# A first batch in halves for sixteen steps only, with the seven-product down projection for all batches

## The chip, the cores and the metric

The kernel runs on one core of a Trainium2 chip. The core has a matrix engine (TensorE, in the profile PE, with its weight loads as PEld), a vector engine (VectorE, DVE), a scalar engine (ScalarE, ACT), a general engine (GpSimd, POOL) and a queue that issues most of the DMA transfers (SyncE, SP). Each engine works through its own instructions in the order in which the program issues them, and waits where an operand isn't there yet. The metric is the device time of one execution in microseconds (us); lower is better. All data are 32-bit floats.

## The reference

There are 8 batches of 512 tokens with 128 channels. Each goes through a linear attention with four heads, and then through eight dense experts that all see every token:

```python
x = x + layernorm(attention(layernorm(x)))      # attention adds its own input, and w_out, b_out
x = x + layernorm(experts(layernorm(x)))

# attention(x): xn = layernorm(x) * gamma + beta; q, k, v = split(xn @ w_qkv)
#   k = softmax(k, axis=tokens); context = k^T v per head; out = (q * 32**-0.5) context
#   return out @ w_out + b_out + x
# experts(x): for wg, wu, wd in the 8 experts:
#   acc += (silu(x @ wg) * (x @ wu)) @ wd       # 128 -> 512 -> 128 channels
```

An expert has 512 hidden channels, so that the eight together make 32 slices of 128. A "step" of the kernel is one such slice for one batch.

## The kernel before

**Steps.** The main loop (lines 962 to 1019) runs over units. A unit is a batch, or half of one, and a range of steps. In a step PE makes `g` (line 976) and `u` (line 978) from the batch's transposed input `zT`, ACT makes `sg`, the Silu of `g` (line 980), and DVE makes `h = sg * u` (line 994, in the last units line 988). `g` and `u` have two PSUM banks each (`ps_gu`), so PE can run ahead of DVE by two steps and no more.

**Down projection.** In units that hold a whole batch, two steps make a pair, and the pair's 2x2 block product is done with seven products in place of eight. POOL makes the needed differences of `h` in the tile `t2` (lines 1014 to 1016, three instructions for a pair), and the sums of the weights were made once into `ws` (`weight_sums`, POOL, line 801). Eight pairs form a group; its products (`down_pairs`, line 863) are issued two steps after the group's last step, on two halves of PE's columns at once, into the banks accA and accB. When a batch's last group is done, `Last` adds the pieces up, in the next batch's steps.

**First batch.** It runs as two units of 256 tokens, each through all 32 steps: 64 half-steps. Its down projection is the plain one (`down`, line 811): one product for each half-step into one bank. At the end of a unit `fT` is copied (line 817) and `finish` (lines 703 to 715) transposes it on PE (line 259), normalises and stores.

**Opening.** Before the loop, `opening` (lines 304 to 428) computes the first batch's attention with all engines, in halves. It runs `after_wa` (lines 660 to 701) as two generators, `first` and `second`: y in PSUM, its statistics (`norm_stats`), `yn`, the residual `x2`, statistics of `x2`, `z`, the transposes and `zT`. `first` is run to its end, since the loop's first g needs its half of zT. `second` is carried on in the loop's first steps. Products called `unread` (`keep_warm`, line 165) fill PE meanwhile.

**Other batches' attention.** For batches from the third on it goes in stages, methods of the class `Attention` (lines 510 to 597), which `plan` (lines 873 to 935) places at numbered steps: for example `keys` at step 1, `context` at 4 to 7, `norm4` and `turn4` at 17. It transposes in 32x32 blocks on DVE and carries the blocks to their places through DRAM, with SP issuing one store and four loads each time (`carry`). The second batch is different: the generator `attention` (lines 430 to 475) gives it one piece at each step of the first batch's second unit, with transposes on PE. `prepare` (lines 143 to 159) and `weight_sums` run in the same way in the first unit.

**Order.** The order of instructions on each engine is the order of the program text, since the schedule is manual. In a step it is: `g`, `u`, Silu, `h`, the calls that `between` (lines 937 to 957) has for this step, the down products that are due, the differences `t2`.

**End.** The last batch runs 24 steps as a whole and the other 8 steps in halves. `End` (lines 717 to 777) adds a half's products token-wise into one PSUM bank. Both tiles of the last half are normalised together in `finish` (lines 753 to 777).

Of the kernel before, what the change touches and what calls it, by code (L numbers as in the profile page):

```python
# [16 lines left out]
def kernel(  # L17
# [40 lines left out]


# [28 lines left out]

    WHOLE, HALVES = [(0, NJ)], [(0, NJ // 2), (NJ // 2, NJ)]
# [21 lines left out]

    wg_sb, wu_sb, wd_sb = [], [], []
    for e in range(E):
        g = const.tile([P, F], F32, name=f"wg_{e}")
        nc.sync.dma_start(g, wg[e])
        u = const.tile([P, F], F32, name=f"wu_{e}")
        nc.sync.dma_start(u, wu[e])
        d = const.tile([P, NF, C], F32, name=f"wd_{e}")
        nc.sync.dma_start(d, wd[e].rearrange("(f p) c -> p f c", p=P))
        wg_sb.append(g)  # L120
        wu_sb.append(u)
        wd_sb.append(d)
        if e == 0 and B > 1:
            xs[1] = load_x(1)

    warm = const.tile([P, N // 2], F32, name="warm")
    nc.vector.memset(warm, 1.0)
# [15 lines left out]
    def prepare():  # L143


        wq_ps = ps.tile([P, N], F32, tag="ps", name="wq_ps")
        nc.tensor.transpose(wq_ps[:, :C], w_qkv_sb[:, 0:C], ident)
        nc.scalar.mul(wqT, wq_ps[:, :C], QSCALE)
        nc.scalar.mul(gwv, w_qkv_sb[:, 2 * C : 3 * C], gamma_sb)
        bv_ps = ps.tile([P, N], F32, tag="ps", name="bv_ps")  # L150
        nc.tensor.matmul(bv_ps[:, :1], w_qkv_sb[:, 2 * C : 3 * C], beta_sb, start=True, stop=True)
        bv = const.tile([P, 1], F32, name="bv")
        nc.scalar.copy(bv, bv_ps[:, :1])
        bvw = const.tile([P, C], F32, name="bvw")
        nc.scalar.mul(bvw, w_out_sb, bv)
        yield
        mb_ps = ps.tile([P, N], F32, tag="ps", name="mb_ps")
        nc.tensor.matmul(mb_ps[:, :C], heads, bvw, start=True, stop=True)
        nc.scalar.copy(mb, mb_ps[:, :C])
# [14 lines left out]
    def norm_stats(src, name):  # L174
# [13 lines left out]
        return mv, rstd  # L188

    def pair_stats(src, name):  # L190
# [15 lines left out]
        if n < NJ:  # L206
            nc.gpsimd.tensor_tensor(rstd[:, n:], ve[:, n:], mhalf[:, :n], ALU.pow)
            return mv, rstd[:, :n], rstd[:, n:], ve
        nc.gpsimd.tensor_tensor(rstd, ve, mhalf, ALU.pow)  # L209
        return mv, rstd[:, :n], rstd[:, n:]  # L210

    def bn(src, name):
        stats = small.tile([P, NJ, 6], F32, tag=f"stats{NJ}", name=f"stats_{name}")
        for j, t in enumerate(pieces(src)):
            nc.vector.bn_stats(stats[:, j, :], t)
        return stats

    def scales(stats, name, pair=False):


# [11 lines left out]
        for i in range(0, n, NJ):  # L232
            nc.vector.tensor_scalar(nm[:, i : i + NJ], mv[:, :, 0], -1.0, None, ALU.mult)  # L233
        rstd = small.tile([P, n], F32, tag=f"srstd{n}", name=f"rstd_{name}")
# [12 lines left out]
    def norm_apply(dst, src, mv_rstd):  # L247
        mv, rstd = mv_rstd
        for j in range(src.shape[1]):
            nc.vector.tensor_scalar(  # L250
                dst[:, j], src[:, j], mv[:, j, 0:1], rstd[:, j : j + 1],
# [47 lines left out]
    def parts(b):  # L299
        return HALVES if b == 0 else WHOLE  # L300

    x2s, zTs, rest = {}, {}, []

    def opening():
# [4 lines left out]
        def bank(name, tag):  # L309
# [13 lines left out]
        y = {}  # L323
# [6 lines left out]
        m = work.tile([P, C], F32, tag="m", name="m_0")  # L330
        first, second = [
            after_wa(b, lo, hi, xt, qT, m, x1b, x2, y, yn, z, zT) for lo, hi in HALVES
# [6 lines left out]
        keep_warm(warm, 4)  # L339
        keep_warm(w_qkv_sb[:, : N // 2])  # L340
        nc.scalar.copy(junk, warm[:, :1])
        s1 = [pair_stats(xt[:, J[h]], f"1_0_{h}") for h in H]
# [60 lines left out]
        nc.scalar.mul(qT[:, COL[0]], q_ps[0][:, :W], QSCALE)  # L403
        ctxT = work.tile([P, C], F32, tag="ctxT", name="ctxT_0")
# [8 lines left out]
        nc.vector.reciprocal(rsum, ksum[:, 2:3])  # L413
        nc.vector.tensor_scalar(m, m_ps[:, :C], rsum, None, ALU.mult)
# [3 lines left out]
        keep_warm(flat(xt[:, J[0]]), 2)  # L418
        next(first)
        next(first)  # L420
        keep_warm(flat(yn[:, J[0]]), 2)
        next(first)
        keep_warm(flat(x2[:, J[0]]), 2)
        next(first)
        next(second)
# [3 lines left out]

    def attention(b):  # L430

        xt = xs[b]
        mv, r1, r2 = pair_stats(xt, f"1_{b}")
        yield
        xh = work.tile([P, NJ, C], F32, tag="xh", name=f"xh_{b}")
        norm_apply(xh, xt, (mv, r2))
        yield
        yield
        xnT = work.tile([P, N], F32, tag="xnT", name=f"xnT_{b}")
        xh_ps = transpose4(flat(xh), f"xh_ps_{b}")  # L440
        nc.scalar.activation(xnT, xh_ps, AF.Identity, bias=beta_sb, scale=gamma_sb)
        yield
        k_ps = ps.tile([P, N], F32, tag="ps", name=f"k_ps_{b}")
        nc.tensor.matmul(k_ps, w_qkv_sb[:, C : 2 * C], xnT, start=True, stop=True)
        kmax = small.tile([P, 1], F32, tag="kmax", name=f"kmax_{b}")
        nc.vector.tensor_reduce(kmax, k_ps, AX.X, ALU.max, negate=True)
        ekT = work.tile([P, N], F32, tag="ekT", name=f"ekT_{b}")
        ksum = small.tile([P, 1], F32, tag="ksum", name=f"ksum_{b}")
        nc.scalar.activation(ekT, k_ps, AF.Exp, bias=kmax, accum_out=ksum)
        yield  # L450
        x1 = work.tile([P, NJ, C], F32, tag="x1", name=f"x1_{b}")
        norm_apply(x1, xt, (mv, r1))
        rsum = small.tile([P, 1], F32, tag="rsum", name=f"rsum_{b}")
        nc.vector.reciprocal(rsum, ksum)
        x1b = x1
        for j in range(NJ):
            nc.gpsimd.tensor_tensor(x1b[:, j, :], x1[:, j, :], bias_sb, ALU.add)  # L457
        yield
        ek = work.tile([P, NQ, P], F32, tag="ek", name=f"ek_{b}")
        ek_ps = transpose4(ekT, f"ek_ps_{b}")  # L460
        nc.vector.tensor_copy(
            ek.rearrange("p b (j k) -> p j b k", j=NJ),
            ek_ps.rearrange("p (j b k) -> p j b k", j=NJ, b=NQ),
        )
        yield
        yield
        yield from to_wa(b, xh, ek, rsum)
        wa = was[b]
        x2 = xp.tile([P, NJ, C], F32, tag="x2", name=f"x2_{b}")
        x2s[b] = x2  # L470
        y = work.tile([P, NJ, C], F32, tag="y", name=f"y_{b}")
        yn = y
        z = work.tile([P, NJ, C], F32, tag="z", name=f"z_{b}")
        zT = zp.tile([P, NQ, NJ, Q], F32, tag="zT", name=f"zT_{b}")
        yield from after_wa(b, 0, NJ, xt, xnT, wa, x1b, x2, y, yn, z, zT)

    was = {}
# [32 lines left out]
    class Attention:  # L510
# [27 lines left out]
        def keys(self):  # L538
# [12 lines left out]
            self.x1 = work.tile([P, NJ, C], F32, tag="x1", name=f"x1_{b}")  # L551
# [40 lines left out]
        def turn4(self):  # L592
# [3 lines left out]
            for lo, hi in parts(b):  # L596
                zTs[b, lo] = zT[:, :, lo:hi]
# [62 lines left out]
    def after_wa(b, lo, hi, xt, xnT, wa, x1b, x2, y, yn, z, zT):  # L660
        r = slice(lo, hi)
        pool, tag = (ps_gu, "u") if b == 0 and lo else (ps, "ps")
        y_ps = pool.tile([P, N], F32, tag=tag, name=f"y_ps_{b}_{lo}")
        if b == 0:
            for j in range(lo, hi):
                cols = slice((j - lo) * C, (j - lo + 1) * C)
                nc.tensor.matmul(y_ps[:, cols], ident, x1b[:, j, :], start=(j == lo), stop=False)
            yield
        for j in range(lo, hi):
            nc.tensor.matmul(  # L670
                y_ps[:, (j - lo) * C : (j - lo + 1) * C], xnT[:, j * P : (j + 1) * P], wa,
                start=(b > 0), stop=(b > 0 or j == hi - 1),
            )
        if b == 0:
            y[lo] = y_ps[:, : (hi - lo) * C].rearrange("p (j c) -> p j c", c=C)
            yb = y[lo]
        else:
            yb = y[:, r]
            nc.vector.tensor_tensor(flat(yb), y_ps[:, : (hi - lo) * C], flat(x1b[:, r]), ALU.add)
        yield  # L680
        s3 = norm_stats(yb, f"3_{b}_{lo}")
        yield
        norm_apply(yn[:, r], yb, s3)
        (nc.gpsimd if b or lo else nc.vector).tensor_tensor(
            flat(x2[:, r]), flat(yn[:, r]), flat(xt[:, r]), ALU.add
        )
        yield
        yield
        s4 = norm_stats(x2[:, r], f"4_{b}_{lo}")
        yield  # L690
        norm_apply(z[:, r], x2[:, r], s4)
        yield
        yield
        z_ps = transpose4(flat(z[:, r]), f"z_ps_{b}_{lo}")
        for j in range(hi - lo if b == 0 and lo == 0 else 1):
            cp = nc.vector.tensor_copy if j else nc.scalar.copy
            if b or lo:
                cp(zT[:, :, r], by_block(z_ps[:, : (hi - lo) * P], hi - lo))
            else:
                cp(zT[:, :, j], z_ps[:, j * P : (j + 1) * P].rearrange("c (a i) -> c a i", a=NQ))  # L700
        zTs[b, lo] = zT[:, :, r]

    def finish(b, lo, hi, fT):

        r = slice(lo, hi)
        n = hi - lo
        f_ps = transpose4(fT, f"f_ps_{b}_{lo}")
        f3 = f_ps.rearrange("p (j b k) -> p j b k", j=NJ, b=NQ)[:, :n]
# [253 lines left out]
    for n, (b, lo, hi, begin, end) in enumerate(units):  # L962
# [55 lines left out]
        for _ in others:  # L1018
            pass
# [36 lines left out]
```

## Time and profile before

Three runs took 704.2, 704.26 and 705.94 us, with a median of 704.26.

| what | value |
|---|---|
| the profiled execution | 705.33 us |
| its span, first to last instruction | 703.5 us |
| around the span | 1.8 us |
| mean granted clock of PE | 0.997 |
| first `g` of the loop starts | 20.34 us |
| first `g` of the second batch | 114.75 us |
| PE's last twelve product instructions start | 696.30 us |
| DVE `h` over 512 tokens, mean of one | 0.688 us |
| DVE `h` over 256 tokens, mean of one | 0.419 us |
| ACT Silu over 512 and 256 tokens, mean of one | 0.598 and 0.383 us |
| POOL power of 2, 4 and 8 columns, mean of one | 0.70, 1.02 and 1.64 us |
| POOL weight sum, 128x128, mean of one | 0.458 us |

A line of the profile's groups has the source line, the engine, the operation, output and inputs by the program's names, shapes and the count; then the busy time in us and the mean of one in ns; then the engine's idle time before it and what ended that. A line of the timeline has the start and the duration in us, the instruction, the count of merged ones, and in brackets the engine's idle time before it with what ended it. A line of the waits has who waited, for whom, the us in total, how often, and the longest. A matmul on 32-bit floats appears as two instructions, so x2 is one product. Durations of matmuls overlap, as they are pipelined; the distance between starts is what one costs in a full stream.

### The profile page before, as it was taken

Reading aid. Unit: us, or ns where it says so; the run is one execution under the profiler, and the core shown is the slowest. Engines: PE = TensorE matmul, PEld = TensorE weight load, DVE = VectorE, ACT = ScalarE, POOL = GpSimd, SP = SyncE. Lnnn points to the kernel's source line nnn. Section 1 sums busy time; section 2 is a strip of 40 time slices with the busy share of each in tenths; the row PEclk is TensorE's granted clock in tenths of the full one; section 3 lists DMA queues with packets and bytes.
Section 4 is the critical chain, followed back from the end, with each engine's and each line's share of the span. In section 5 each row is a group of like instructions: output and inputs, shape, how many; then the busy total and the mean of one; then the engine's idle time right before and its main releaser. Section 6 shows DMA issues by size and latency. Waiting matters only on the chain.

```text
span 703.5 us, 9130 instructions
## 1 busy us (share of the span) xinstructions
PE 690.5 (98%) x3161; PEld 397.5 (56%) x3161; DVE 297.5 (42%) x815; ACT 243.8 (35%) x472; POOL 386.1 (55%) x481
## 2 busy tenths in 40 slices
PE   8998999999999999999999999999999999999996
PEld 6787886455464545545455454555445454544576
DVE  5534463553424633364324634256242543235134
ACT  3332435324423434143342433324342323122221
POOL 3711120875737767385754857367663766546521
PEclk9999999999999999999999999999999999999999
DMA  8400001102011110202001020111101010020010
GB/s 266 157 1 0 8 0 51 32 1 75 0 48 43 54 39 20 63 8 89 1 31 60 2 91 0 31 60 32 46 0 65 26 47 1 0 61 1 15 56 20
DMA packets 33214, 28.19 MB, mean 40 GB/s; under 512 B 3600, under 2 KB 25360, under 8 KB 33168
## 3 DMA queue, kind: packets, MB, share of 16 engines
q1 hardware_dynamic: 32880, 27.41, 12.2%
q8 instruction: 25, 0.41, 0.3%
q10 hardware_dynamic: 288, 0.20, 0.1%
q14 instruction: 21, 0.17, 0.1%
HBM read 17.11 MB, written 10.49 MB: 39 GB/s over the span
## 4 chain that ended last, share of the span: by engine, by line
PE 94%; issue 2%; DVE 2%; POOL 1%; ACT 1%; DVEq 0%; POOLq 0%
PE g L976 31%; PE u L978 30%; PE accA L863 13%; PE accB L863 10%; PE acc L811 3%; PE acc L733 1%; PE y_ps L566 1%; PE g_ps L483 1%; PE k_ps L541 1%; PE unread L165 1%; POOL rstd L187 0%; DVE stats L181 0%; PE z_ps L259 0%; POOL x L457 0%; POOL rstd L209 0%
## 5 line engine op out<-in xcount | busy, mean ns | idle before, releaser
L994 DVE TENSOR_TENSOR h<-sg,u 128x512 f32<-128x512 f32 (+1 forms) x280 | 175.1, 626 | 356.2 <-PE u L978 340.9
L980 ACT ACTIVATE sg<-g 128x512 f32<-128x512 f32 (+1 forms) x296 | 159.5, 540 | 393.1 <-PE g L976 371.3
L976 PE MATMUL g<-zT,wg 128*128 128x512 f32 (+1 forms) x592 | 270.6, 539 | 0.9 <-DVE zT L700 0.7
L978 PE MATMUL u<-zT,wu 128*128 128x512 f32 (+1 forms) x592 | 268.9, 536 | 0.2 <-DVE h L994 0.2
L1014 POOL TENSOR_TENSOR t<-h 128x512 f32<-128x512 f32 x108 | 137.4, 1272 | 140.6 <-DVE h L994 140.6
L978 PEld LDWEIGHTS u<-zT,wu 128*128 128x128 f32 x592 | 112.4, 190 | 108.7 <-issue 100.9
L976 PEld LDWEIGHTS g<-zT,wg 128*128 128x128 f32 x592 | 107.9, 191 | 91.7 <-issue 86.2
L863 PE MATMUL accB<-t,ws 128*64 128x256 f32 x432 | 120.4, 381 | 0.0
L863 PE MATMUL accA<-h,wd 128*64 128x256 f32 x432 | 111.6, 381 | 0.0
L1016 POOL TENSOR_TENSOR t<-h,t 128x256 f32<-128x256 f32 x108 | 78.6, 727 | 8.5
L1015 POOL TENSOR_TENSOR t<-h,t 128x256 f32<-128x256 f32 x108 | 78.5, 727 | 8.5
L863 PEld LDWEIGHTS accA<-h,wd 128*64 128x64 f32 x432 | 58.0, 137 | 39.3 <-issue 5.6
L863 PE MATMUL accA<-t,ws 128*64 128x256 f32 x216 | 64.2, 379 | 0.0
L863 PE MATMUL accB<-h,ws 128*64 128x256 f32 x216 | 64.2, 379 | 0.0
L863 PEld LDWEIGHTS accB<-t,ws 128*64 128x64 f32 x432 | 58.0, 137 | 0.0
L235 POOL TENSOR_TENSOR rstd<-ve,mhalf 128x4 f32<-128x4 f32 (+1 forms) x24 | 28.1, 1171 | 23.0 <-DVE nm L233 15.6
L811 PE MATMUL acc<-h,wd 128*128 128x256 f32 x128 | 38.6, 383 | 0.0
L863 PEld LDWEIGHTS accB<-h,ws 128*64 128x64 f32 x216 | 29.6, 137 | 15.6
L863 PE MATMUL accB<-t,wd 128*64 128x256 f32 x108 | 32.1, 379 | 0.0
L863 PE MATMUL accA<-t,wd 128*64 128x256 f32 x108 | 32.1, 379 | 0.0
L187 POOL TENSOR_TENSOR rstd<-ve,mhalf 128x2 f32<-128x2 f32 (+1 forms) x9 | 7.0, 773 | 41.9 <-DVE ve L185 41.7
L863 PEld LDWEIGHTS accA<-t,ws 128*64 128x64 f32 x216 | 29.6, 137 | 0.0
(189 smaller groups left out, 455.9 us busy)
## 6 DMA issues: line engine op xcount, KB each, us to landing
wg<-in_L_ffn_Wg_dram SPq DMA_DIRECT2D x8, 256.0 KB, 6.0
wu<-in_L_ffn_Wu_dram SPq DMA_DIRECT2D x8, 256.0 KB, 5.9
wd<-in_L_ffn_Wd_dram SPq DMA_DIRECT2D x8, 256.0 KB, 6.1
x<-in_L_attn_x_dram SPq DMA_DIRECT2D x7, 256.0 KB, 3.1
bounce<-f_blkA SPq DMA_DIRECT2D x7, 256.0 KB, 2.0
fA<-bounce SPq DMA_DIRECT2D x28, 64.0 KB, 2.0
bounce<-f_blkB SPq DMA_DIRECT2D x7, 256.0 KB, 2.1
fB<-bounce SPq DMA_DIRECT2D x28, 64.0 KB, 2.0
```

What stands on the lines that cost most here:

```text
L165: nc.tensor.matmul(t[:, : moving.shape[1]], moving[:, :P], moving, start=(i == 0), stop=(i == count - 1),)
L235: nc.gpsimd.tensor_tensor(rstd, ve, mhalf[:, :n], ALU.pow)
L483: nc.tensor.matmul(g_ps[:, :C], xh[:, j, :], ek[:, :, j * Q : (j + 1) * Q], start=(j == 0), stop=(j == NJ - 1),)
L811: nc.tensor.matmul(accs[n][:, :cols], wd_sb[e][:, f, :], h, start=(i == 0), stop=(i == NSTEP - 1))
L863: nc.tensor.matmul(o, w, r, start=start, stop=stop)
L976: nc.tensor.matmul(g_ps[:, :cols], wg_sb[e][:, w], zT, start=True, stop=True)
L978: nc.tensor.matmul(u_ps[:, :cols], wu_sb[e][:, w], zT, start=True, stop=True)
L980: nc.scalar.activation(sg[:, :cols], g_ps[:, :cols], AF.Silu)
L994: nc.vector.tensor_tensor(h, sg[:, :cols], u_ps[:, :cols], ALU.mult)
L1014: nc.gpsimd.tensor_tensor(t2[:, 0:2], h2[:, 1::2], h2[:, 0:2], ALU.subtract)
L1015: nc.gpsimd.tensor_tensor(t2[:, 2], h2[:, 3], t2[:, 0], ALU.subtract)
L1016: nc.gpsimd.tensor_tensor(t2[:, 3], h2[:, 2], t2[:, 2], ALU.subtract)
```

## The change

1. The units of the first batch become: each half through steps 0 to 15, then the whole batch through steps 16 to 31.
2. Its down projection is by pairs with seven products. The first group's pairs are filled by both halves (`h2s`), the differences are made when the second half's step is there, and the group's products come after step 17. `down`, `finish` and `by_block` copies of `fT` are gone; `Last` finishes the batch in the second batch's steps.
3. In the half-steps, which have no down product, every third step takes accA and accB for `g` and `u`.
4. The second batch's attention is an `Attention` as well. Its statistics are made in `opening`; the stages are placed in the first batch's steps. x of the second batch is loaded ahead of the experts' weights. `bias` is split off from `keys`.
5. `prepare` runs in `opening`, in one bank. Weight sums of experts 0 to 4 are on POOL at steps 2, 4, 6, 8, 10; those of 5 to 7 on DVE at step 17.
6. `after_m` takes the variance of `x2` from the variances of its two parts and their covariance, instead of a second pass of statistics over `x2`.
7. The last half's two tiles have a bank each (accA, accB), and their normalisation goes tile by tile.
8. The constant 1.0 takes the place of the tile `warm`, and the first `keep_warm` makes five products.

```diff
+    xs[1] = load_x(1)
     for e in range(E):
...
-        if e == 0 and B > 1:
-            xs[1] = load_x(1)
-    warm = const.tile([P, N // 2], F32, name="warm")
-    nc.vector.memset(warm, 1.0)
+    warm = nc.const_aps.tensor(1.0, (P, N // 2), F32)
...
+        after = attentions[1] = Attention(1)            # in opening, after qT of half 0
+        after.s = bn(after.x[:, :3], "1_1")
...
+        bn(after.x[:, 3:], "1_1", after.s, 3)           # ahead of m
...
-        keep_warm(flat(xt[:, J[0]]), 2)
+        moment = moments(after.s, "1_1", pair=True)
+        weights = prepare()
+        next(weights)
+        keep_warm(flat(xt[:, J[0]]))
         next(first)
+        next(weights)
+        keep_warm(flat(xt[:, J[0]]))
         next(first)
-        keep_warm(flat(yn[:, J[0]]), 2)
+        next(weights)
         next(first)
-        keep_warm(flat(x2[:, J[0]]), 2)
-        next(first)
-        next(second)
+        after.sc = powers(*moment, "1_1")
+        keep_warm(flat(yn[:, J[0]]), 2)
+        next(first)
         for _ in first:
             pass
         rest.append(second)
...
+        mvx, vex = s1[h][0], s1[h][3]                   # in after_m
+        cov, rv, t, rstd2 = small2
+        mv, rstd, ve = norm_stats(y, f"3_0_{lo}", keep=True)
+        yield
+        for j in range(n):
+            nc.vector.scalar_tensor_tensor(
+                z[:, lo + j], xt[:, lo + j], mvx[:, j, 0:1], y[:, j], ALU.subtract, ALU.mult,
+                accum_out=cov[:, j : j + 1],
+            )
+        nc.vector.tensor_scalar(cov, cov, 2.0 / C, None, ALU.mult)
+        nc.vector.reciprocal(rv, ve)
+        nc.vector.tensor_tensor(rv, rv, mv[:, :, 1], ALU.mult)
+        nc.vector.tensor_tensor(rv, rv, vex[:, :n], ALU.add)
+        nc.gpsimd.tensor_tensor(t, rstd, cov, ALU.mult)
+        nc.gpsimd.tensor_tensor(t, t, rv, ALU.add)
+        nc.gpsimd.tensor_tensor(rstd2, t, mhalf[:, :n], ALU.pow)
+        yield
+        norm_apply(yn[:, r], y, (mv, rstd))
...
+        norm_apply(z[:, r], x2[:, r], (mvx, rstd2))
...
-    units = [(b, lo, hi, 0, NSTEP) for b in range(B - 1) for lo, hi in parts(b)]
-    units.append((B - 1, 0, NJ, 0, SPLIT))
+    units = [(0, lo, hi, 0, GROUP) for lo, hi in HALVES] + [(0, 0, NJ, GROUP, NSTEP)]
+    units += [(b, 0, NJ, 0, NSTEP if b < B - 1 else SPLIT) for b in range(1, B)]
     units += [(B - 1, lo, hi, SPLIT, NSTEP) for lo, hi in HALVES]
...
+        if b == 0 and begin == 0:                       # in plan
+            if not lo:
+                second = rest.pop()
+                go = lambda: next(second, None)
+                at(0, go, a.norm)
+                at(1, go)
+                at(3, a.turn)
+                at(4, go)
+                at(6, go)
+                at(8, go)
+                for i, e in enumerate((0, 1, 2, 3, 4)):
+                    at(2 + 2 * i, lambda e=e: weight_sums(nc.gpsimd, [e]))
+                at(9, a.bias)
+                at(13, a.affine)
+                at(14, a.keys)
+            else:
+                for i in range(12, 16):
+                    at(i, a.context)
+            return p
...
+            at(16, a.values)                            # whole unit of the first batch
+            at(17, a.stats3, a.scales3, second.stats, second.scales, a.residual)
+            at(17, lambda: weight_sums(nc.vector, [5, 6, 7]), second.norm, second.turn)
+            at(19, a.stats4)
+            at(20, a.scales4)
+            at(22, a.norm4, a.turn4)
+            at(24, second.affine)
...
+            spare = b == 0 and not whole and count % 3 == 2
+            g_ps, u_ps = (
+                ps_acc.tile([P, N], F32, tag=f"acc{s}", name=f"{t}_{n}_{i}") if spare
+                else ps_gu.tile([P, N], F32, tag=t, name=f"{t}_{n}_{i}")
+                for t, s in ("gA", "uB")
+            )
...
+                if lo == 0 and i % 2 == 0:
+                    h2s.append(pairp.tile([P, 4, N // 2], F32, tag="h2", name=f"h2_{n}_{i}"))
+                h2 = h2s[-1] if whole else h2s[i // 2]
+                k = 2 * (i % 2) + (lo > 0)
+                h = h2[:, k : k + 2] if whole else h2[:, k : k + 1]
+                nc.vector.tensor_tensor(flat(h), sg[:, :cols], u_ps[:, :cols], ALU.mult)
+            made = not last and i % 2 and hi == NJ
...
+            s = [norm_stats([f], f"5_{b}_{self.lo + j}") for j, f in enumerate(self.f)]   # End.finish
+            for j, f in enumerate(self.f):
+                norm_apply([fn[:, j]], [f], s[j])
```

In the fence, notes behind a `#` name the function that a piece is in.

## The prediction

> **What bounds the kernel now.** First the busy shares, then the stretches, then the waits of TensorE (PE).
>
> ```profile
> PE 690.5 (98%) x3161; PEld 397.5 (56%) x3161; DVE 297.5 (42%) x815; ACT 243.8 (35%) x472; POOL 386.1 (55%) x481
> ```
> ```profile
> 20.00:114.70 94.70, 91.04 (x425) 77.44 (x426) 43.99 (x147) 32.37 (x81) 25.00 (x46) 0.98 0.10 31
> 114.70:700.00 585.30, 582.55 (x2663) 308.42 (x2662) 240.95 (x616) 204.98 (x378) 352.65 (x411) 1.00 0.11 34
> ```
> ```profile
> PE f_ps L259 <- DVE fT L817: 3.2, 2, 2.7
> PE g L976 <- DVE zT L700: 0.7, 1, 0.7
> PE z_ps L259 <- DVE z L250: 0.6, 2, 0.5
> ```
>
> The second fence gives, for each stretch, its length and then the busy time of PE, weight loads, DVE, ACT and POOL, the granted clock and the DMA share. PE sets the end: it works 98% of the span, and from 126 us to the last steps the trace shows no wait of PE at all. The first batch (20 to 114.7 us) is the stretch with idle PE. So the change is worth what it takes out of PE's instruction stream, plus the waits that it removes in the first 126 us, less the waits that it makes. The spacing of PE's starts prices both:
>
> ```profile
> 94.92 0.59 PE L976 MATMUL g<-zT,wg 128*128 128x256 f32 x2
> 95.35 0.59 PE L978 MATMUL u<-zT,wu 128*128 128x256 f32 x2
> 95.78 0.59 PE L811 MATMUL acc<-h,wd 128*128 128x256 f32 x2
> 96.21 0.59 PE L976 MATMUL g<-zT,wg 128*128 128x256 f32 x2
> ...
> 115.61 1.02 PE L978 MATMUL u<-zT,wu 128*128 128x512 f32 x2
> 116.46 0.59 PE L811 MATMUL acc<-h,wd 128*128 128x256 f32 x2
> ```
> ```profile
> 151.36 0.43 PE L863 MATMUL accA<-h,wd 128*64 128x256 f32 x1
> ...
> 154.44 0.38 PE L863 MATMUL accA<-h,wd 128*64 128x256 f32 x1
> ```
>
> Starts are 0.431 us apart for a product over 256 tokens, 0.859 for one over 512. Two pairs of the seven-product form start at 151.36 and the next two at 154.44, so a pair takes 1.54 us.
>
> **The sum, part by part** (gains positive).
>
> *Down projection of the first batch.* Before: 64 products of 0.431 = 27.6 us. After: 16 pairs of 1.54 = 24.6. **+3.0.** This is less than an eighth: a pair in plain form is 4 x 0.431 = 1.73, and seven products on two half-arrays take 1.54.
>
> *Sixteen steps over 512 tokens instead of twice sixteen over 256.* Per step 2 x 0.859 = 1.718 against 4 x 0.431 = 1.726: **+0.1.** Halves cost PE nearly nothing.
>
> *PE work that leaves the loop.* The second batch goes through DVE's block transposes and DMA, as later batches do, so its transposes xh, ek and z (four of 0.11 each, 0.44 us each set) go, with those of the two finishing halves (f, 0.44), and prepare's products (0.25 at 21.31, 0.33 at 22.72) move into the opening, where PE waits anyway: **+2.3.**
>
> *Waits that go.* I compare start-to-start distances with the spacings above. Around f_ps at 65:
>
> ```profile
> 65.14 0.59 PE L978 MATMUL u<-zT,wu 128*128 128x256 f32 x2
> 68.41 0.69 PE L259 MATMUL f_ps<-ident,fT 128*128 128x128 f32 x2 [2.67 <-DVE fT L817]
> 68.89 1.06 PE L811 MATMUL acc<-h,wd 128*128 128x256 f32 x2
> 69.75 1.06 PE L976 MATMUL g<-zT,wg 128*128 128x256 f32 x2
> 70.60 0.95 PE L978 MATMUL u<-zT,wu 128*128 128x256 f32 x2
> 71.39 0.60 PE L259 MATMUL xh_ps<-ident,xh 128*128 128x128 f32 x4
> ```
>
> The wait costs 2.84, and the four groups behind it run 0.26, 0.43, 0.42 and 0.36 late, at a granted clock of 0.52 between 68.4 and 71.4. Together 4.3. In the same way: 0.5 at 78.9, 1.2 at the z transposes (96.7 to 98.8), 1.1 at the second f and the Silu behind it (120.8 to 124.7), 0.2 at 22. **+7.3.**
>
> *New waits in the first sixteen half-steps.* Without the down product a half-step lasts only 0.863, so PE leans on DVE, ACT and POOL. I laid out the four queues by their order in the changed program, with durations of the rows (h 0.42, Silu 0.38, normalising 4x128 on ACT 1.65, block transpose 0.71, pow 0.70 for 2 columns and 1.64 for 8, weight sums 4 x 0.46). From the first g as zero:
> - DVE has h and the statistics of the second half (about 1.0) behind step 0, then the new covariance: two scalar_tensor_tensor with an accumulated sum. No such DVE instruction is in the trace. Nearest row: scalar_tensor_tensor m at 0.34, so 0.7 for two; with a separate accumulator read as ACT's (0.19), 1.1; far end 1.3. I take 1.0, plus four small ones of 0.2. h of step 2 comes late, and u of step 5, which needs its bank, waits **1.0**.
> - POOL does the pow of 8 columns, the second half's three small ones and pow, then expert 0's sums (1.84), and only then x2 of the second half, at 8.1. DVE's z waits for it, then z_ps at step 8: **0.7** with u of step 8. Queued behind z on DVE are h of 7 and 8.
> - keys at step 14: ACT loads the Exp table (1.28), exp 0.88, loads Silu again (1.28); Silu of step 15 ends about 5.0 after Silu of 14 began, DVE's h behind kmax and the transpose. PE can run three steps ahead, since every third step takes the spare banks; g of count 18 waits **1.0**. k_ps itself waits 0.15 for the affine.
> Sum **-2.9**. Bounds: zero if my hand-off times are too long; -6 if DVE is 25% slower than its rows while POOL works beside it (the queues laid out again with that).
>
> *The differences t2 of the first group.* POOL makes eight sets while PE runs sixteen half-steps of 0.86.
>
> ```profile
> L1014 POOL TENSOR_TENSOR t<-h 128x512 f32<-128x512 f32 x108 | 137.4, 1272 | 140.6 <-DVE h L994 140.6
> L1016 POOL TENSOR_TENSOR t<-h,t 128x256 f32<-128x256 f32 x108 | 78.6, 727 | 8.5
> L1015 POOL TENSOR_TENSOR t<-h,t 128x256 f32<-128x256 f32 x108 | 78.5, 727 | 8.5
> ```
>
> A set is 1.27 + 0.73 + 0.73 = 2.73 us, a pair of half-steps 1.73. POOL starts at 20.8 and ends at 42.6; PE reaches the products at 37.5 and needs the last two sets 9.2 later, at 46.7. Four us of slack: **0**. The Trainium skill, GPSIMD Engine Reference, Engine selection, speaks against this placement: element-wise work belongs on VectorE, two-input operations being about twice as slow on GpSimd. The row agrees in size (1.27 for 512 elements against 0.69 for h on DVE), but DVE's full queue is what makes PE wait here; by the rule one would move 22 us of POOL work to 12 on the engine that is late. By rule a loss, by these rows nothing.
>
> *The stages at steps 16 to 24.* Three experts' sums on DVE (12 x 0.28 = 3.4), two sets of statistics and a transpose fill DVE for about 10 us at step 17, POOL's pow waits behind the eight sets; both lie beside the 12.3 us of products. h and Silu of step 18 are ready about 3 us before. Without that cover DVE's 10 us would show. The bounces on SP (a store, four loads, about 6 us) start ten or more steps ahead of use, behind the last weight loads; the second batch's zT lands eight us before its step. Weight loads: expert 3 is wanted at about 30 us and was issued by 11. **0.**
>
> *Opening.* Removed: second statistics on x2 (0.49 + 0.30 + 0.17), pow 0.7 with hand-offs. Added on DVE: covariance 1.8, the second batch's moments 1.3 (0.9 fits in the wait before y_ps), x's bn_stats, which fit the idle 0.74 and 0.32. rstd2 on POOL runs beside yn and x2. First g moves from 20.34 to about 20.15; a fifth warm-up product may cost 0.2 at 5 us. **0**, bounds -0.7 to +0.6.
>
> *Tail.* The last half's two tiles get separate banks, so statistics of the first start 0.44 earlier and pow of one column follows (about 0.55): **+0.6**, bounds 0 to 0.8.
>
> Total 3.0 + 0.1 + 2.3 + 7.3 - 2.9 + 0.6 = **10.4**. The profiled execution took 705.33 (span 703.5 and 1.8 around it): 694.9. It lies 1.1 above the median of the runs, 704.26; against that, **694.0**.
>
> The clock is where a second rule bears. The Trainium skill, TensorE: Matmul & The Clock Gate, Part 1, says that PE falls to half rate after an idle window of some 3.4 us and needs as long busy to recover. The row is stricter: 2.7 us of waiting was followed by 0.52 and cost 1.5 beyond the wait. My new waits are at most 1.0; by the rule and by the row they cost no clock, though 1.0, 0.7 and the slow spots between them fall within 6 us. If they count as one, 1.5 more.
>
> **Rivals.**
> 1. As summed: 694.0. Chance 0.62.
> 2. The first sixteen half-steps are dearer (DVE slowed by POOL, covariance 1.3, a clock dip): -6 instead of -2.9, opening -0.7: 697.8. For it: POOL is busy there without a break, and z rows reached 0.61 beside it. Against: h beside POOL from 126 us on keeps 0.69. 0.16.
> 3. The waits are covered by banks and queue: 691. 0.12.
> 4. Slower: POOL's sets are late, PE stands at the first group. From 20.8 to the limit 46.7 there are 25.9 us for eight sets; beyond it PE stands for the rest. The whole gain is gone at (25.9 + 10.4)/8 = 4.5 us a set; at twice the row, 5.5 us, PE stands 18 and the kernel takes about 712. For it: the backlog is real, 7 us when the half-steps end. Against: the same three shapes, 108 times at 2.73. 0.04.
> 5. The seven-product form saves nothing and both 2 and the opening go wrong: 701. 0.06.
>
> Range 690.5 to 699. A difference under 0.3% (2.1 us) can't be told from none: faster 0.93, same 0.02, slower 0.05.
>
> **What would show it.** Right: no f_ps or fT; products of group 0 with no POOL wait; first g within 0.5 of 20.2; second batch's first g at about 94 (114.75 now); PE's waits before it at u of step 5, z_ps, and g behind Silu 15, under 4 in sum. Wrong: PE waiting on t2, a granted clock below 0.9 after 20 us, or waits of PE above 5 in the first batch.

## The result, and the profile after

The changed kernel took **693.47 us** (median of four runs, 693.28 to 693.53), beside 704.23 for the kernel before (704.16 to 705.94). The ratio is 0.984, with a 95% interval of 0.982 to 0.986. The kernel before runs at two levels, near 704.1 and near 705.8 us, and its profiled execution is one of the upper level (last section). The profiled execution of the changed kernel took 693.51 us with a span of 691.6, so against the profiled execution of before (705.33, 703.5) the span is 11.9 us shorter.

The busy shares of the changed kernel:

```profile
PE 682.9 (99%) x3175; PEld 374.3 (54%) x3175; DVE 298.3 (43%) x810; ACT 247.9 (36%) x475; POOL 424.6 (61%) x524
```

PE is 7.6 us less busy, and POOL 38 us more: the differences `t2` of the first batch are new there (16 sets, 42.8 us in the two traces), while the weight sums of three experts (5.6 us), which POOL made before, went over to DVE. The stretches of the changed kernel, from its first `g` on (length, busy time of PE, weight loads, DVE, ACT and POOL, granted clock, DMA share):

```profile
20.00:56.00 36.00, 34.43 (x161) 27.58 (x160) 20.67 (x59) 19.64 (x47) 27.92 (x46) 1.00 0.26 83
56.00:96.00 40.00, 40.00 (x178) 20.09 (x177) 20.75 (x63) 15.08 (x29) 32.38 (x38) 1.00 0.11 33
```

From 56 to 96 us PE has no idle time, and the granted clock is 1.00, where before it was 0.98 over the first batch. What is left of waits is in the half-steps and the opening. The waits of PE:

```profile
PE u L903 <- DVE h L926: 0.9, 2, 0.7
PE unread L161 <- PEq L966: 0.8, 1, 0.8
PE g L902 <- ACT sg L905: 0.7, 1, 0.7
PE g L902 <- DVE zT L673: 0.7, 1, 0.7
PE xh_ps L350 <- DVE xh L252: 0.2, 1, 0.2
```

There is no f_ps, z_ps or POOL among them. The line of `L902 <- DVE zT` is the first g of the loop, which starts at 19.53 (20.34 before). The second batch's first g starts at 93.26 (114.75 before):

```profile
19.53 0.70 PE L902 MATMUL g<-zT,wg 128*128 128x256 f32 x2 [0.68 <-DVE zT L673]
...
93.26 1.02 PE L902 MATMUL g<-zT,wg 128*128 128x512 f32 x2
```

The 11.9 us of span, by the start-to-start distances of PE in both traces: 2.8 from seven products (measured below), 0.1 from whole steps, 2.3 from transposes and preparation that left PE's stream, 7.3 from waits that went, 0.8 from the opening, 0.55 from the tail (from the last common product to the end 6.65 instead of 7.2), less 2.1 for new waits. That is 11.75. The 0.1 and the 2.3 are taken over from the forecast, where they were worked out from the spacings in the trace of before; the other parts are read from the traces or measured.

### The profile page after: what moved, and what is told of

It is laid out like the page before. It is cut to its first block, busy times and chain, and to the rows that moved or that the text cites. A ratio compares the mean times of both kernels' runs of the same rounds, so it can differ in the third digit from the quotient of the medians.

```text
span 691.6 us, 9214 instructions
## 1 busy us (share of the span) xinstructions
PE 682.9 (99%) x3175; PEld 374.3 (54%) x3175; DVE 298.3 (43%) x810; ACT 247.9 (36%) x475; POOL 424.6 (61%) x524
## 4 chain that ended last, share of the span: by engine, by line
PE 96%; DVE 1%; ACT 1%; DMA 0%; issue 0%; POOL 0%; DVEq 0%; ACTq 0%
PE g L902 32%; PE u L903 31%; PE accA L797 16%; PE accB L797 12%; PE y_ps L528 1%; PE g_ps L443 1%; PE k_ps L501 1%; PE end L699 1%; DMA x<-in_L_attn_x_dram 0%; PE end_A L699 0%; ACT xh L245 0%; PE wa_ps L464 0%; PE end_B L699 0%; PE m_ps L458 0%; PE c_ps L452 0%
## 5 line engine op out<-in xcount | busy, mean ns | idle before, releaser
L902 PE MATMUL g<-zT,wg 128*128 128x512 f32 (+1 forms) x560 | 267.5, 559 | 1.4 <-ACT sg L905 0.7
L940 POOL TENSOR_TENSOR t<-h 128x512 f32<-128x512 f32 x124 | 157.2, 1268 | 158.4 <-DVE h L926 158.4
L902 PEld LDWEIGHTS g<-zT,wg 128*128 128x128 f32 x560 | 101.2, 190 | 98.9 <-issue 95.6
L797 PE MATMUL accB<-t,ws 128*64 128x256 f32 x496 | 138.2, 381 | 0.0
L797 PE MATMUL accA<-h,wd 128*64 128x256 f32 x496 | 128.1, 381 | 0.0
L941 POOL TENSOR_TENSOR t<-h,t 128x256 f32<-128x256 f32 x124 | 90.1, 726 | 9.7
L942 POOL TENSOR_TENSOR t<-h,t 128x256 f32<-128x256 f32 x124 | 90.0, 726 | 9.7
L797 PEld LDWEIGHTS accA<-h,wd 128*64 128x64 f32 x496 | 66.6, 137 | 45.2 <-issue 6.4
L797 PE MATMUL accB<-h,ws 128*64 128x256 f32 x248 | 73.8, 379 | 0.0
L797 PE MATMUL accA<-t,ws 128*64 128x256 f32 x248 | 73.8, 379 | 0.0
L797 PEld LDWEIGHTS accB<-t,ws 128*64 128x64 f32 x496 | 66.6, 137 | 0.0
L797 PEld LDWEIGHTS accB<-t,wd 128*64 128x64 f32 x124 | 17.0, 137 | 9.0
L516 POOL TENSOR_TENSOR x<-x,bias_sb 128x128 f32<-128x128 f32 x28 | 11.9, 455 | 15.3 <-ACT x L245 15.3
```

Source lines behind the costliest of these rows:

```text
L516: nc.gpsimd.tensor_tensor(self.x1[:, j], self.x1[:, j], bias_sb, ALU.add)
L797: nc.tensor.matmul(o, w, r, start=start, stop=stop)
L902: nc.tensor.matmul(g_ps[:, :cols], wg_sb[e][:, w], zT, start=True, stop=True)
L940: nc.gpsimd.tensor_tensor(t2[:, 0:2], h2[:, 1::2], h2[:, 0:2], ALU.subtract)
L941: nc.gpsimd.tensor_tensor(t2[:, 2], h2[:, 3], t2[:, 0], ALU.subtract)
L942: nc.gpsimd.tensor_tensor(t2[:, 3], h2[:, 2], t2[:, 2], ALU.subtract)
```

## The experiments

All times are medians; the changed kernel is 693.47.

**The seven products alone (e2_plain).**

```diff
             below, above = [], []
+            if b == 0:
+                for m, (h, t) in enumerate(pairs[two : two + 2]):
+                    ...
+                        (A[:, left], w0, h[:, 0], k == 0, False),
+                        (A[:, right], w1, t[:, 2], False, k == last),
+                        (D[:, left], w0, t[:, 1], k == 0, False),
+                        (D[:, right], w1, t[:, 3], False, k == last),
+                continue
```

> The changed kernel, with four plain products over the full array for each pair of the first batch in place of seven on half arrays (its first batch's sums are then not the reference's; the differences are still made and read). By the sum on record a pair takes 1.73 in place of 1.54 us, so +3.0: 696.5 against 693.5. Rival, the seven-product form saves nothing here since PE waits for others at these places: 693.5.

Measured: 696.22 us (696.20 to 696.40), so the form is worth 2.75. This kernel leaves out the right sums of the first batch, but makes as many products as the plain form. In the traces the way from the u ahead of the first group to the g behind it takes 14.68 instead of 13.19, which is 1.5 for each of the two groups. The forecast's 3.0 (27.6 less 24.6; unrounded 2.94) holds within 0.2.

**The spare banks (e3_nospare).**

```diff
-            spare = b == 0 and not whole and count % 3 == 2
+            spare = False
```

> The changed kernel without accA and accB as a third pair of banks in the half-steps, so that PE can run ahead by two steps and not three. If the new waits come from late h and Silu, each wait grows: in the four queues laid out with the measured durations PE loses 1.7 us more, most of it (0.9) ahead of the g that waits for Silu of step 15: 695.2. Rival, the banks don't bound PE and its waits come from elsewhere: 693.5.

Measured: 695.87 us (695.80 to 696.01), 2.4 more. The waits of PE in it:

```profile
PE g L902 <- ACT sg L905: 1.6, 1, 1.6
PE u L903 <- DVE h L926: 1.3, 4, 0.6
```

The wait behind the Silu of step 15 is 1.6 instead of 0.7: one step less that PE can run ahead is one g and u (0.86) more of waiting. The rest of the 2.4 are mostly waits of u, of which the expectation had too little. By start-to-start distances the u's of steps 1 to 5 wait 2.3 together, one after the other, where two of them waited 1.2 before; a further 0.3 is a g near 33 us. Why it is these five is found further down (e11).

**POOL's sets made longer (e4_poolslow).** The first of a set's three instructions is issued twice in the half-steps.

```diff
-                nc.gpsimd.tensor_tensor(t2[:, 0:2], h2[:, 1::2], h2[:, 0:2], ALU.subtract)
+                for _ in range(2 if b == 0 and not whole else 1):
+                    nc.gpsimd.tensor_tensor(t2[:, 0:2], h2[:, 1::2], h2[:, 0:2], ALU.subtract)
```

> The changed kernel, with the first of POOL's three instructions issued twice for the eight sets of the first group, so that a set takes 4.0 us in place of 2.73. By the prediction POOL has about 4 us of slack over eight sets: 8 x 1.27 = 10.2 more, of which 6.2 reach PE, as waits of the products of the third and the fourth two pairs (1.2 and 4.9): 699.7. Rival, no slack, the products wait for POOL already: +10, 703.7. Rival, more slack than thought: under 696.

Measured: 700.46 us (700.28 to 700.69), 7.0 more, close to the expectation. The products of the first group in it that wait, and ahead of them one that runs without a partner:

```profile
66.09 0.59 PE L797 MATMUL accA<-h,wd 128*64 128x256 f32 x2
68.28 0.43 PE L797 MATMUL accB<-t,ws 128*64 128x256 f32 x1 [1.59 <-POOL t L941]
69.09 0.43 PE L797 MATMUL accA<-t,ws 128*64 128x256 f32 x1 [0.15 <-POOL t L942]
72.63 0.43 PE L797 MATMUL accB<-t,ws 128*64 128x256 f32 x1 [1.96 <-POOL t L941]
```

The waits in brackets add up to 3.7, but the group takes 17.89 from its start to the next g instead of 12.24, which is 5.65 more. All of it lies in the last two pairs, which take 8.78 (66.09 to 74.87) instead of 3.12; the expectation had a part of it, 1.2, in the two pairs before. By start-to-start distances the waits there come to 4.6. Most of the rest is lost overlap: four products (at 66.09, 69.57, 70.02 and 74.35) run on one half of PE's columns with nothing beside them, where in the changed kernel the products go in twos. Side by side the four would take two stretches of 0.43 less, an estimated 0.9. Another 0.95 is a g that waits for a Silu, which stands behind normalisations that wait for POOL. So the slack of POOL was real and finite, as the slower rival had it: at 4.3 us a set (8 sets from 39.90 to 74.14) two thirds of the gain are gone.

**The differences on DVE (e5_t2dve).** This puts the rule of the Trainium skill (GPSIMD Engine Reference, 4.1 Engine selection) to the test: element-wise work on VectorE, not on GpSimd.

```diff
-                nc.gpsimd.tensor_tensor(t2[:, 0:2], h2[:, 1::2], h2[:, 0:2], ALU.subtract)
+                eng = nc.gpsimd if whole else nc.vector
+                eng.tensor_tensor(t2[:, 0:2], h2[:, 1::2], h2[:, 0:2], ALU.subtract)
...
```

> The changed kernel with the differences of the first group's pairs (h2 of the two halves) on DVE instead of POOL; all else as it is. The forecast costed these sets on POOL at nothing, since POOL had 4 us to spare; the Trainium skill's rule (GPSIMD Engine Reference, 4.1 Engine selection) speaks for DVE. Theory (DVE is the engine that frees PE's banks in this stretch, and every set put on it, three instructions of together some 1.5 us, stands ahead of the h of a later step): PE waits at u after every second of the second half's steps, about 0.7 us each, in sum 5.3, so 698.8 us. Rival 1, the rule as it reads (the faster engine is the better one): 693.5 or a little less. Rival 2 (DVE has enough idle time, 47 of 74 us busy): no change, 693.2 to 693.8.

Measured: 697.80 us (697.67 to 697.87), 4.3 more. The waits of PE in it:

```profile
PE u L903 <- DVE h L926: 1.8, 5, 0.7
PE c_ps L452 <- DVE gs L448: 1.5, 1, 1.5
PE unread L161 <- PEq L967: 0.8, 1, 0.8
PE g L902 <- ACT sg L905: 0.7, 1, 0.7
PE g L902 <- DVE zT L673: 0.7, 1, 0.7
PE wa_ps L464 <- DVE m L460: 0.5, 1, 0.5
```

Each instruction is faster on DVE (0.69 + 0.43 + 0.43 us for a set, against 1.27 + 0.73 + 0.73 on POOL), and yet the kernel is slower: `gs` and `m` of the attention and the h of every second step now come behind a set, and PE stands for them. The size is near the theory's 5.3, the places only in part: by start-to-start distances three u's wait some 0.5 each, while c_ps and wa_ps, which the theory did not have, wait 2.4 together. The second rival's 47 us are the weight loads' column; DVE was busy for 40.5 of the 74.5 us, so its idle time was larger still, and did not help.

**The covariance undone (e6_stats).**

```diff
+        mv, rstd = norm_stats(y, f"3_0_{lo}")
...
+        s4 = norm_stats(x2[:, r], f"4_0_{lo}")
+        yield
+        norm_apply(z[:, r], x2[:, r], s4)
```

> The changed kernel with one part undone: the statistics of x2 in the opening are again taken from x2 itself by bn_stats and bn_aggr, instead of from the covariance. The forecast set the opening's gain to 0 (bounds -0.7 to +0.6); the profile of the changed kernel shows its first product 0.8 us earlier. Theory (the 0.8 us come from the covariance, whose two instructions and accumulator reads took 0.62 us beside other work): the first product comes 1.1 to 1.4 us later, 694.6 to 694.9 us. Rival (the 0.8 us come from the order and placing of the rest of the opening, the covariance gives nothing): 693.2 to 693.8.

Measured: 694.33 us (694.14 to 694.58), 0.9 more; its first g starts at 20.60, 1.07 later. The rival falls, and the size is a little below the expectation, as some of the DVE work left in the half-steps goes too: PE's wait of 0.9 for h near 24 us is absent and 0.3 at z_ps is there instead. The rest of the opening's changes cost 0.26 (20.60 against 20.34 in the kernel before), so the covariance is worth 1.07 and the opening 0.81. The part that the forecast had left at nothing, in the changed kernel's timeline, and then `yn` in kernel e6:

```profile
15.16 0.34 DVE L648 SCALAR_TENSOR_TENSOR z<-x,mv,y_ps 128x128 f32<-128x128 f32 x1
15.33 0.71 POOL L183 TENSOR_TENSOR rstd<-ve,mhalf 128x2 f32<-128x2 f32 x1 [3.10 <-DVE ve L181]
...
15.43 0.08 DVE L648 DVE_READ_ACCUMULATOR z<-x,mv,y_ps 128x1 f32 x1
15.43 0.34 DVE L648 SCALAR_TENSOR_TENSOR z<-x,mv,y_ps 128x128 f32<-128x128 f32 x1
...
16.35 0.73 DVE L252 TENSOR_SCALAR yn<-y_ps,mv,rstd 128x128 f32<-128x128 f32 x2
```
```profile
16.00 0.73 DVE L252 TENSOR_SCALAR yn<-y_ps,mv,rstd 128x128 f32<-128x128 f32 x2 [0.82 <-POOL rstd L183]
```

The two with their reads take 0.62 us (15.16 to 15.78), in a time in which DVE without them waits 0.82 for POOL's `rstd`. With the four small instructions behind them they put `yn` off by only about 0.3 (16.35 against 16.00).

**The waits of before moved (e1_later).** The kernel before, with the attention of the second batch three steps later.

```diff
+        for _ in range(3):              # in attention(), ahead of pair_stats
+            yield
```

> The kernel before, with the second batch's attention begun three half-steps later, so that the copy fT of the first half is ahead of its norm on DVE. By the sum on record, the wait of PE ahead of f_ps at 65 us and the slow clock behind it cost 4.3 us; both go: about 700.0 us against 704.2, with the clock at 1.0 through 60 to 80 us. Rival, the wait only moves (DVE and POOL have the same work to do, and another product waits for it): less than 1.5 us faster, above 702.7.

Measured: 703.92 us (20 runs, 703.64 to 704.12), ratio to before 0.998 (0.9975 to 0.9988). The kernel before took 705.71 beside it, 1.8 more, since 14 of its 23 runs there were on the upper level; against its lower level, near 704.1, the gain is about 0.2. So the 4.3 did not come, and the rival, that the wait only moves, held. The wait of 2.7 us at f_ps is gone, but the sum of waits and slow spots is 5.4 instead of 7.3, with new ones of 1.3 at 71.9 and 1.1 at 103.7. Moving the attention of before does not remove its waits. In the changed kernel the instructions that waited are gone: the transposes are off PE, and the half-steps have no down products. Which of these two took off how much was not measured. The other thing that it shows stands in the last section.

**Where the new waits come from: five kernels.** The wait of u near 24 us is the largest that the change made. The timeline of the changed kernel there, DVE and PE:

```profile
22.82 0.34 DVE L648 SCALAR_TENSOR_TENSOR z<-x,mv,y_ps 128x128 f32<-128x128 f32 x1
...
23.50 0.59 PE L902 MATMUL g<-zT,wg 128*128 128x256 f32 x2
...
24.01 0.75 DVE L926 TENSOR_TENSOR h<-sg,u 128x256 f32<-128x256 f32 x2
...
24.82 0.70 PE L903 MATMUL u<-zT,wu 128*128 128x256 f32 x2 [0.72 <-DVE h L926]
```

The g at 23.50 is that of step 4. Its u waits for the h of step 3, which together with that of step 2 stands behind the covariance (22.82 to 24.09). Three ideas of a better order:

```diff
# e7_spread: plan of the first half
+                at(2, go)
+                at(4, a.turn)
+                ...
+                at(10, go)
# e8_split: in after_m, behind the scaling of cov; and one more piece in the plan
+        if lo:
+            yield
+                at(2, go)
# e9_split2: as e8, and keys() cut behind kmax, its rest called exps()
-                at(13, a.affine)
-                at(14, a.keys)
+                at(12, a.affine)
+                at(13, a.keys)
+                at(14, a.exps)
```

> The changed kernel with the small work of the first half's steps moved: the second half's attention pieces at steps 0, 2, 6, 8 and 10 instead of 0, 1, 4, 6 and 8, the second batch's transposes at 4 instead of 3, and the expert sums on POOL at 2, 6, 8, 10 and 12. No work is added or left out. Theory (the wait of 0.9 us at u near 24 us is DVE doing the attention's piece ahead of an h): that wait goes, 692.6 us. Rival (the pieces push the second half's start or a later bank, and the wait turns up there): 693.2 to 693.8, or more.

> The changed kernel with the second half's covariance in two pieces: its two products with their accumulator reads and the scaling stay at step 1 of the first half, the reciprocal and what follows goes to step 2, so that an h stands between them on DVE. Theory (the 0.9 us wait of u near 24 us is the length of this block of 1.3 us of DVE ahead of an h, not its place): the wait shrinks to 0.1 to 0.3, 692.7 to 692.9 us. Rival (any DVE work in these steps comes out at the same h's, as when the pieces were spread): 693.3 to 693.9.

> As the kernel with the split covariance, and the second batch's keys in two pieces a step earlier: affine at step 12 instead of 13, the product k_ps and the maximum at step 13, Exp and the transposes at 14 as before. Theory (of the 3.7 us in which ACT makes no Silu near 36 us, 0.37 are Exp waiting for the maximum): the wait of g near 38 us shrinks from 0.9 to about 0.5, 692.3 to 692.5 us. Rival (the two loads of ACT's tables set that stretch alone): as the split alone, 692.7 to 692.9.

Measured: 693.94 (693.79 to 694.10), 693.80 (693.61 to 693.85) and 694.24 us (694.12 to 694.37). None gains, and the theory of each falls. With the pieces spread, the wait of u is 0.99 and a further one of 0.3 follows at 27; with the covariance in two it is again 0.89. e9 fails for another reason: k_ps (0.86 us of PE work) had stood in the stretch in which ACT makes no Silu, and a step earlier it no longer fills it. From kernel e9, and then from the changed kernel:

```profile
33.50 1.13 PE L501 MATMUL k_ps<-xnT,w_qkv_sb 128*128 128x512 f32 x2
...
35.50 1.28 ACT L511 ACT_TABLE_LOAD   x1
...
39.32 0.70 PE L911 MATMUL g<-zT,wg 128*128 128x256 f32 x2 [1.24 <-ACT sg L914]
```
```profile
34.25 1.12 PE L501 MATMUL k_ps<-xnT,w_qkv_sb 128*128 128x512 f32 x2
...
34.49 1.28 ACT L506 ACT_TABLE_LOAD   x1
...
38.67 0.70 PE L902 MATMUL g<-zT,wg 128*128 128x256 f32 x2 [0.70 <-ACT sg L905]
```

The outage of ACT is 0.37 shorter, the cover 0.86 shorter; the wait goes from 0.87 to 1.40 start to start.

What the orders have in common is that a u waits for the h just one step before it. u has two banks and every third step takes accB, so the u of step 4 should wait for the h of step 1. The second half's `y_ps` holds one of them: `pool, tag = (ps_gu, "u") if lo else (ps, "ps")` (line 627), until yn is made from it (25.96 to 26.68). The kernel before has the same line (662), so in its first steps too u had one bank, not two; in its trace no u waited there. That gave one more theory, and two kernels on it:

```diff
# e11_ybank
-        pool, tag = (ps_gu, "u") if lo else (ps, "ps")
+        pool, tag = ps, "ps"
# e12_ybank10: the same, and
-                at(8, go)
+                at(10, go)
```

> The changed kernel with the second half's y_ps in the bank pool ps instead of in u's. Nothing else is moved, the order of all instructions is the same. Theory (in the first half's steps u has only one bank of its two, since y_ps holds the other until yn is made near 26.5 us; so the u of a step waits for the h of the one before, and it is this that makes the waits of 0.3 us near 21 and 0.9 near 24, whatever DVE's order): both waits go, 692.1 to 692.4 us. Rival 1 (the waits are the length of DVE's work, and any bank waits for them): 693.2 to 693.6. Rival 2 (ps has no bank free then, so y_ps itself or the transposes z_ps start later): over 693.6.

> As the kernel with the second half's y_ps in pool ps, and the transposes z_ps at step 10 of the first half instead of 8. There both waits of u had gone (1.2 us), but PE, then 1.2 us ahead, waited 1.1 us at z_ps for z. Theory (z_ps is only early in PE's order; z is ready near 29 us): no wait of PE from 20 to 37 us, 692.2 to 692.5 us. Rival (the time is given back again later, at the start of the second half's steps or at k_ps and Exp): 693.2 to 693.5.

Measured: e11 693.50 us (693.18 to 693.51), e12 **692.60 us** (692.43 to 692.73; ratio to before 0.982, 0.981 to 0.984). The time of e11 is no different, and yet the cause was found: both waits of u are gone, with the same instructions in the same order. Only a u of step 5 waits, 0.1. The bank fits e3 as well, where each u from step 1 to step 5 waited, and none behind yn (26.59 to 27.32 there). By its time alone e11 reads as its first rival; the trace decides against that one. PE is 1.2 us ahead at step 8 and now waits at z_ps, where the changed kernel arrived too late to wait:

```profile
27.72 0.99 DVE L252 TENSOR_SCALAR z<-x,mv,cov 128x128 f32<-128x128 f32 x2 [0.73 <-POOL x L661]
...
28.32 0.77 PE L261 MATMUL z_ps<-ident,z 128*128 128x128 f32 x2 [0.54 <-DVE z L252]
```

The z itself starts at the same time in both (27.70 in the changed kernel, 27.72 here). By start-to-start distances 0.71 of waiting lies before z_ps and 0.39 behind it, 1.1 together. With z_ps two steps later the waits of e12 are these, and no u or z_ps is among them:

```profile
PE unread L161 <- PEq L966: 0.8, 1, 0.8
PE g L902 <- ACT sg L905: 0.7, 1, 0.7
PE g L902 <- DVE zT L673: 0.7, 1, 0.7
```

The changed kernel once more, beside e8 and e9:

> The changed kernel itself, once more beside the others. Theory: 693.3 to 693.6 us, with no two levels, while the kernel before again shows two, near 704.1 and 705.8.

Measured: 693.31 us (693.24 to 693.58). Together with its first four runs no run of the changed kernel is below 693.24 and none of e12 above 692.73, so e12 is faster than the changed kernel by 0.7 to 0.9 us (0.1%). The runs were not side by side, and the difference is small; but the traces show it too: the g behind the keys starts at 37.88 instead of 38.67.

## Why the prediction was right, step by step

- **Down projection, +3.0:** 2.75 measured (e2). Right. Against plain pairs, seven products save about a tenth (2.75 of 27.6), not an eighth.
- **Whole steps +0.1, PE work that leaves +2.3:** no experiment took these alone; the account of the span closes with them within 0.2, which bears them out but does not show each.
- **Waits that go, +7.3:** right for the profiled execution that the sum was made against, as none of these waits is left. But 1.5 of it, the slow clock behind f_ps, seems to belong to part of the executions only (last section). To take the same 1.1 from both ends ("against that, 694.0") was not sound, since the change removes this very excess: the gain should have been taken from the profile and the time left at the sum's 694.9. The subtraction itself slipped by 0.1: 704.26 less 10.4 is 693.9, not 694.0.
- **New waits, -2.9:** 2.1 measured. The keys' wait was right (1.0 forecast, 0.87, at g of count 18). The waits at u and z_ps were misread. Forecast were 1.0 at u of step 5, for a bank behind the covariance, and 0.7 at z_ps, added up. In the trace they are 0.3 at u of step 1 and 0.9 at u of step 4, and none at z_ps: my layout gave u two banks, where y_ps holds one (e11). And the two are alternatives: the delay at u is what lets z come in time, and without it z_ps waits 1.1 (e11). e11, which has the two banks of my layout, shows what that layout was worth: z_ps waits 0.7 as forecast and 0.4 behind it, but the u of step 5 waits 0.1 and not 1.0. Both edits together gain (e12); z_ps two steps later without the other bank was run only among other moves (e7), with no gain.
- **t2 at nothing:** right. No product waited for POOL, whose eight sets ended at 62.64, 3.4 us before the last two pairs began (66.00); four were forecast. e4 shows where the slack ends.
- **Engine selection:** the Trainium skill's rule, weighed in the forecast as a loss, would have lost 4.3 us here (e5). Its factor of about two for the single instruction agrees with e5's rows (0.69 against 1.27).
- **Stages at nothing:** right, no wait of PE after 40 us.
- **Opening, 0:** wrong by 0.8. The term that was mis-sized is the covariance. The forecast set 1.8 of new DVE work against 1.66 that goes, as if all of it lay on the way to the first g. The two instructions with their reads took 0.62 instead of 1.0, and as they ran beside POOL's pow the whole put `yn` off by about 0.3; e6 gives the exchange 1.07. The bound of +0.6 was too narrow as well.
- **Tail, +0.6:** 0.55 in the traces; no experiment took it alone.

So the sum was 1.4 short against the profiled execution (0.8 in the opening, 0.8 in the new waits, less 0.25 in the products), and the shift to the median took off 0.9. The forecast was 0.5 us from the result since these nearly cancel; its mechanism was right, that it came so close was luck.

## What to carry to other kernels

When a step's products lose their filling work, count the free banks that each of them really has, with every other tile that lives in the pool, before laying out queues. Waits one behind another on an engine are not to be added: the first may be what hides the second, so an edit that removes one alone shows no gain and is not refuted by that. Here an engine that is slower per instruction but had slack was the better place for work that would otherwise stand ahead of what PE waits for.

## What was not expected of the hardware

Over all runs in this study, the kernel before falls into two groups with nothing between: 29 executions at 703.84 to 704.43 us and 32 at 705.50 to 706.11, at mean granted clocks of 0.997 to 1.000 and 0.995 to 0.997. e1, which removes its longest wait, has 20 of 20 at 703.64 to 704.12, and its clock over the stretch of the first batch is whole:

```profile
20.00:114.70 94.70, 92.07 (x429) 77.09 (x430) 44.25 (x147) 33.37 (x83) 24.88 (x46) 1.00 0.10 32
```

All eight runs of the changed kernel lie within 0.35 us. So the wait of 2.7 us seems to slow the clock in about every second execution, which pays 1.7 us for it. The Trainium skill (TensorE: Matmul & The Clock Gate, Part 1) puts the idle window at some 3.4 us; in the trace of before a wait of 2.67 was followed by a clock of 0.52, and the measurement decides. That the clock holds in the other executions is inferred: the 1.7 fits the 1.5 us that the profile showed behind f_ps, but there is no trace of an execution in the lower group, so the link is borne out by e1 rather than shown. If it holds, it is also why e1 gained less than its sum: nearly all that it saves is this clock, and only in every second run.
